# Graph attention on a sparse adjacency matrix: 384 rows ranked early, their q made in part one

## The chip, the cores and the metric

The kernel runs on one core of one Trainium2 chip. The metric is the device time of one execution in microseconds (us). The engines are TensorE (PE, with PEld for its weight loads), VectorE (DVE), ScalarE (ACT), GpSimd (POOL) and SyncE (SP), which here only issues DMAs. Each engine works through a queue of its own in order.

## The reference

`x` is 3327 x 1024 and fp32, `adj` a symmetric 3327 x 3327 matrix of 0 and 1 with ones on the diagonal, about 0.5% of it ones (17 in a row on average).

```python
h = relu(layernorm(x))
f = h @ Wf + bf;  g = h @ Wg + bg        # 1024 x 1024 weights
e = relu(f @ g.T)
scores = where(adj > 0, e, -9e15)
out = x + softmax(scores, axis=1) @ (h @ W + bW)
```

## The kernel before, in words

Only the scores of neighbours are needed. With A = Wf·Wg^T a score is q·h, where q = h_i·A belongs to the row and h to the neighbour. And softmax times (hW + bW) is (softmax times h)·W + bW. So each row needs its list of neighbours, its q (three thirds of 342 columns, the last holding a bias), one dot per neighbour, a softmax, the weighted sum of the same neighbour rows, and one product with W.

**Part one** (to about 240 us) goes over 26 tiles of 128 rows (the last has 127). For each tile the adjacency is loaded; ACT counts its ones (the degrees), POOL multiplies a mask with column numbers (`r<-r,iotaj`, L704), DVE takes the eight largest of each of 16 segments (`MAX8`, L767, function `segments`) and packs them into a list of up to 24 neighbours (`listed`, stored to `pd` through `pay`); what is left over for rows of higher degree goes to `cd` (`cand`, function `store_left`, L747). Besides, each tile of x is normalised (`measured`, `rooted`, `inverted`, `scaled`, `store_h`: the steps of a layer norm on ACT and DVE, then a store by SP to `hd`), and PE multiplies the weights to A (L837), one step of a list per tile. `emptied1` holds the copies that ACT has to make of finished banks, and `empty()` makes them.

At the end of part one the rows are sorted by degree: PE counts with one-hot matrices how many rows of a degree stand before each row (`before`, `after` into `pre`), DVE makes ranks from it, and 26 more matmuls turn ranks into `perm`, the row number at each rank. SP stores the last lists and the last leftover lists after that.

**Part two** goes over 26 tiles of sorted rows, in the order of `ORDER`. `CAPS` holds how many neighbours a tile has at most. The steps of a tile `t` are: `L` fetches its lists, `H` its own rows (both indirect gathers on POOL, made by `gather`, L639); PE turns the rows (`hT`, L1239) and multiplies them by A (`q`, L1246), ACT copies the bias ahead (`fq`) and the thirds behind (`qc`); `G` gathers one neighbour row for each of the 128 rows into one of `ROWS` row buffers; `d` is a dot on DVE (L1259); `S`, `A`, `E`, `Y`, `T` are the softmax. The weighted sum is made in two ways: `s` on DVE (L1312), or `w` on ACT (L1295, scales the row) and `p` on PE (L1299, adds it transposed). `SHARE` says how many of a tile's rows go the second way. Then PE multiplies with W (`W`, L1327), `X` adds x to the result by a gather, `O` scatters the tile to the output. `C` and `F` fetch the leftover lists (`cts`) and find the neighbours in them for the two tiles with more than 24; `x` fetches the x rows of the last tile into a row buffer. `fl` is a flag that all rows fitted their lists (L1361).

The order in each engine's queue is written by a planner when the program is built. `steps_of` lists each step with its engine, its cost, the steps that it waits for and, for some, a time before which it is not to start. `forward` plays them through: an engine that is free takes, of the steps that can run, the one with the lowest rank; `FREE_AT` says when each engine is done with part one. `backward` re-ranks, 30 passes are made, and the best plan sets the queues and the row buffer of each gather. Between engines only semaphores order the work on the chip; a step whose time the planner misjudged holds what stands behind it in its queue.

```python
FREE_AT = {"POOL": 247.6, "PE": 268.5, "ACT": 268.4, "DVE": 246.0, "DMA": 247.0}
...
        add("POOL", 1.31, 1.31, ("L", t), ("M", t - 3), *(("G", t - 3, k) for k in range(CAPS[ORDER[t - 3]] if t > 2 else 0)))
```

## Time and profile before

| what | before |
|---|---|
| three runs | 1223.2, 1229.3, 1235.4 us (median 1229.3) |
| the profiled execution | 1226.98 us, of which the span is 1225.2 |
| mean granted clock of TensorE | 0.966 |
| DVE busy | 1116.6 us, 91% |
| PE busy | 1098.0 us, 90% |
| POOL busy | 942.2 us, 77% |
| ACT busy | 602.7 us, 49% |

The span runs from the first to the last instruction of the profiled execution. An engine counts as busy while an instruction of its own runs; a wait on a semaphore isn't busy. A matmul's end is modelled. In the views, `G<-hd,ps` is an indirect DMA that gathers rows of `hd` by the list `ps` into row buffers, L639 is the line of the helper that makes it, and "<-ACT q L1128" behind a wait names what ended it. The same steps have other lines in the changed kernel: `gather` L656, dots L1400, thirds of q L944 in part one and L1387 in part two.

### The profile page before, as it was taken

The numbers are of one execution on the slowest core, as the hardware profiler recorded it, in microseconds if no ns is written. First come the engines' busy times: TensorE is split into PE (matmuls) and PEld (weight loads), VectorE is DVE, ScalarE is ACT, GpSimd is POOL, SyncE is SP. The second block draws the span as 40 slices with busy tenths as digits, with TensorE's granted clock in tenths as the row PEclk, the third lists the DMA queues.
The fourth block names the chain that finished last, engine by engine and source line by source line (L and its number), as shares of the span: only waits on it lengthen the run. The fifth ranks groups of instructions, "written<-read, shape, count | busy, mean of one in ns | idle before, by whom it ended". The sixth has DMA issues, their size and how long they took to land. (4 is left out here: it accounts for less than half of the span.)

```text
span 1225.2 us, 14006 instructions
## 1 busy us (share of the span) xinstructions
PE 1098.0 (90%) x4508; PEld 697.0 (57%) x4508; DVE 1116.6 (91%) x2191; ACT 602.7 (49%) x924; POOL 942.2 (77%) x677
## 2 busy tenths in 40 slices
PE   2799990799939899899999999999899999999997
PEld 2566660466628466556665666655465656555553
DVE  5999998659898999999999999898999999999983
ACT  6899887325617355436543365443332434333351
POOL 8999997277677787878888878777787888877841
PEclk9899995799979999999999999999899999999999
DMA  9999999689888999989999998888988989998962
GB/s 369 420 398 396 397 356 338 199 318 339 280 259 278 333 308 316 347 273 326 305 331 316 321 310 299 289 285 296 314 285 284 312 275 320 295 315 258 326 183 54
DMA packets 101913, 374.43 MB, mean 306 GB/s; under 512 B 14859, under 2 KB 18602, under 8 KB 98631
## 3 DMA queue, kind: packets, MB, share of 16 engines
q0 software_dynamic: 79584, 286.77, 69.9%
q1 hardware_dynamic: 22246, 86.68, 18.7%
q8 instruction: 37, 0.61, 0.2%
q14 instruction: 46, 0.38, 0.1%
HBM read 344.11 MB, written 29.30 MB: 305 GB/s over the span
## 5 line engine op out<-in xcount | busy, mean ns | idle before, releaser
L639 POOL DMA_INDIRECT G<-hd,ps x454 | 569.2, 1254 | 152.6 <-issue 96.9
L1259 DVE CUSTOM_DVE_ANT_0 junk<-G,q 128x1024 bf16<-128x1024 f32 x468 | 564.2, 1225 | 35.5 <-DMA G<-hd,ps 21.1
L1327 PE MATMUL p_o<-W_sb,yT 128*128 128x512 f32 x832 | 365.7, 593 | 3.7 <-ACT yT L1323 3.7
L1312 DVE SCALAR_TENSOR_TENSOR G<-G,sc 128x1024 f32<-128x1024 f32 (+1 forms) x281 | 354.8, 1263 | 6.1 <-ACT G L1284 5.4
L1246 PE MATMUL p_q<-A_sb,hT 128*128 128x342 f32 x1152 | 350.3, 455 | 8.7 <-ACT p_q L1255 7.3
L1246 PEld LDWEIGHTS p_q<-A_sb,hT 128*128 128x128 f32 x1152 | 214.4, 191 | 117.0 <-issue 10.0
L1327 PEld LDWEIGHTS p_o<-W_sb,yT 128*128 128x128 f32 x832 | 155.1, 189 | 187.9 <-issue 177.1
L1299 PE MATMUL p_y<-ident,G 128*128 128x128 f32 x1552 | 189.3, 276 | 15.1 <-DVE G L1312 8.3
L1299 PEld LDWEIGHTS p_y<-ident,G 128*128 128x128 f32 x1552 | 174.9, 142 | 43.1 <-ACT G L1295 13.5
L704 POOL TENSOR_TENSOR r<-r,iotaj 128x1664 f32<-128x1664 f32 (+3 forms) x50 | 184.0, 3750 | 3.4 <-ACT r L697 3.4
L1295 ACT ACTIVATE G<-G,sc 128x1024 f32<-128x1024 f32 x168 | 179.1, 1137 | 0.1
L837 PE MATMUL ps_A<-WgT,WfT 128*128 128x342 f32 x432 | 129.7, 458 | 2.4 <-ACT WfT L832 2.4
L767 DVE MAX8 cand<-r 128x8 f32<-128x208 f32 (+2 forms) x416 | 118.9, 360 | 4.2 <-POOL r L704 3.6
L1338 ACT ACTIVATE xp<-p_o,rs 128x512 f32<-128x512 f32 x50 | 34.2, 686 | 174.3 <-PE p_o L1327 131.2
L837 PEld LDWEIGHTS ps_A<-WgT,WfT 128*128 128x128 f32 x432 | 81.3, 192 | 42.3 <-ACT WfT L832 2.5
L697 ACT ACTIVATE r<-r 128x3327 f32<-128x3327 int32 (+3 forms) x27 | 77.3, 2864 | 12.1 <-DMA r<-in_adj_dram 12.1
L1252 ACT COPY q<-p_q 128x342 f32<-128x342 f32 x72 | 31.5, 441 | 103.7 <-PE p_q L1246 74.3
L639 POOL DMA_INDIRECT xp<-in_x_dram,perm x25 | 49.4, 1974 | 19.9 <-ACT xp L1338 13.2
L1280 ACT ACTIVATE sc<-sc,nm 128x10 f32<-128x10 f32 (+10 forms) x36 | 10.9, 303 | 106.2 <-DVE nm L1270 86.6
L1242 ACT COPY hT<-p_t 128x512 f32<-128x512 f32 x48 | 27.3, 585 | 72.3 <-PE p_t L1239 42.9
L1323 ACT COPY yT<-p_y 128x512 f32<-128x512 f32 x52 | 30.0, 586 | 59.9 <-PE p_y L1299 59.9
L1345 POOL DMA_INDIRECT out_dram<-xp,perm x25 | 31.3, 1252 | 35.8 <-DMA xp<-in_x_dram,perm 30.9
(147 smaller groups left out, 724.6 us busy)
## 6 DMA issues: line engine op xcount, KB each, us to landing
r<-in_adj_dram SPq DMA_DIRECT2D x24, 1663.5 KB, 13.1
xt<-in_x_dram SPq DMA_DIRECT2D x22, 512.0 KB, 13.6
hd<-xt SPq DMA_DIRECT2D x22, 512.0 KB, 10.5
G<-hd,ps POOLq DMA_INDIRECT x454, 6.1
A_sb<-in_L_gnn_Wg_dram SPq DMA_DIRECT2D x8, 512.0 KB, 17.1
A_sb<-in_L_gnn_Wf_dram SPq DMA_DIRECT2D x8, 512.0 KB, 12.0
W_sb<-in_L_gnn_W_dram SPq DMA_DIRECT2D x8, 512.0 KB, 6.4
cd<-cand SPq DMA_DIRECT2D x25, 64.0 KB, 12.6
```

The source lines that it names most:

```text
L639: return nc.gpsimd.indirect_dma_start(out=to, out_offset=None, in_=table, in_offset=bass.IndirectOffsetOnAxis(ap=idx, axis=0), **kw,)
L697: nc.scalar.activation(r[:n, b:e], a[:n, b:e], AF.Sign, accum_out=to)
L704: eng.tensor_mul(r[:n, b:e], r[:n, b:e], iotaj[:n, b:e])
L767: nc.vector.max(cands[t][:n, s * 8 : s * 8 + 8], r[:n, s * SW : min(N, (s + 1) * SW)])
L837: nc.tensor.matmul(ps[:, :QB], WfTs[c][:, k, :], WgT[:, k, o : o + QB], start=(k == 0), stop=(k == KD - 1))
L1246: nc.tensor.matmul(ps_q[(3 * t + i) % 2][:, :QB], hT[:, k, :], A_sb[:, k, i * QB : (i + 1) * QB], start=False, stop=(k == KD - 1), skip_gr ...
L1259: nc.vector.tensor_tensor_reduce(junks[k % 2], row(t, k), q[:, :D], 1.0, 0.0, op0=ALU.mult, op1=ALU.add, accum_out=scs[t % 3][:, k : k + 1],)
L1295: nc.scalar.activation(g, g, AF.Copy, scale=scs[t % 3][:, k : k + 1])
L1299: nc.tensor.matmul(ps_y[g][:, c, :], of[:, (4 * g + c) * P : (4 * g + c + 1) * P], ident, is_transpose=True, start=((t, g) not in begun an ...
L1312: nc.vector.scalar_tensor_tensor(y, row_k, scs[t % 3][:, k : k + 1], y, op0=ALU.mult, op1=ALU.add)
L1327: nc.tensor.matmul(ps_o[o], yT[:, k, :], W_sb[:, k, o * CB : (o + 1) * CB], start=False, stop=(k == KD - 1), skip_group_check=True,)
L1338: nc.scalar.activation(to, ps_o[o], AF.Copy, scale=rss[t % 3])
```

## The change

Of the first eight tiles (`GROUP`) of part one, the 384 rows with ranks 384 to 767 by degree among themselves are chosen while part one is running (`greater`, `early_ranks`, `early_rows`, at its steps 10 to 12). They are tiles 25, 24 and 23 of the sorted order, and these are the first three of `ORDER`; all other rows are ranked as before, without them. Their lists are fetched by POOL in the middle of part one, their own rows at step 22, and their q is made by PE in the tail of part one: `turns` is a list of turns and thirds, and each `go()` makes the next one and fills banks ahead for two thirds. `QN` is 3, so q is kept for three tiles; `ROWS` is 25, the index buffers `pis` are fixed, and `iotaq` lies in the buffer of W, whose last five parts are loaded later. The 26 rank matmuls of the end stay; in front of them, counting of the last four tiles is made at once (`several`). `measured(22)` is made by DVE instead of ACT, and half of the segments of tile 23 are scanned later. The planner gets new constants and new times, and the tiles have new caps (471 rows in sum instead of 468) and shares (176 instead of 168).

```diff
-CAPS = [37, 25, 23, 22, 21, 21, 20, 20, 19, 19, 18, 18, 17, 17, 17, 16, 16, 15, 15, 15, 14, 14, 13, 13, 12, 11]
-ORDER = [24, 15, *range(15), *range(16, 24), 25]
-SHARE = [9, 11, 18, 12, 10, 9, 10, 8, 7, 7, 8, 8, 5, 8, 4, 4, 4, 4, 3, 3, 3, 2, 3, 0, 5, 3]
+CAPS = [38, 25, 23, 22, 21, 21, 20, 20, 19, 19, 18, 18, 17, 16, 16, 15, 15, 14, 14, 13, 13, 12, 11, 18, 17, 16]
+GROUP = 8
+FROM = 384
+EARLY = 3
+ORDER = [25, 24, 23, *range(15), 16, 17, 18, 15, 19, 20, 21, 22]
+SHARE = [14, 14, 10, 17, 15, 13, 10, 10, 7, 5, 10, 5, 9, 4, 7, 7, 0, 2, 0, 3, 5, 2, 2, 4, 1, 0]
...
+QN = 3
+STORED = 233.0
+Q_AT = [214.0, 229.0, 244.0]
...
-ROWS = 26
+FREED = [16, 17, 1, 2, 3, 4, 5, 21, 22, 0, 23, 24, 6, 7, 20, 8, 9, 10, 11, 15, 18, 19, 12, 13, 14]
+ROWS = 25
...
+PINS = {("H", EARLY): 0.0, ("H", EARLY + 1): 1.0}
+FREE_AT = {"POOL": 207.0, "PE": 241.0, "ACT": 237.0, "DVE": 243.0, "DMA": 207.0}
-FREE_AT = {"POOL": 247.6, "PE": 268.5, "ACT": 268.4, "DVE": 246.0, "DMA": 247.0}
...
-        if t > 1:
-            add("POOL", 1.31, 1.31, ("H", t), row=True)
+        if t >= EARLY:
+            add("POOL", 1.31, 1.31, ("H", t), row=True, at=STORED)
...
-                    *(("d", t - 2, k) for k in range(CAPS[ORDER[t - 2]])), *(("S", t - 2, c) for c in range(2) if i == 2),
+                    *(("d", t - QN, k) for k in range(CAPS[ORDER[t - QN]])),
+                    *(("S", t - QN, c) for c in range(2) if i == 2),
...
-                late = [("F", t)] if k >= KL else [("hc", 2, 1) if k < 6 else ("qc", 2, 1)] if t == 1 else []
-                add("POOL", 1.31, 1.31, ("G", t, k), ("Ld", t), *late, row=True)
+                late = [("F", t)] if k >= KL else []
+                add("POOL", 1.31, 1.31, ("G", t, k), ("Ld", t), *late, row=True, at=STORED)
                 add("DMA", 1.33, 3.2, ("Gd", t, k), ("G", t, k))
                 add(
-                    "DVE", 1.148, 1.32, ("d", t, k), ("Gd", t, k), *(("qc", t, i) for i in range(3)),
-                    ("M", t), at=(256.0, 266.0)[t] if t < 2 else 0.0,
+                    "DVE", 1.148, 1.32, ("d", t, k), ("Gd", t, k), *hs, ("M", t), at=Q_AT[t] if t < EARLY else 0.0,
...
+        def greater():
+            nc.vector.tensor_tensor(
+                more_than,
+                iotad[:, None, :].to_broadcast([P, GROUP, NBIN]),
+                deg[:, :GROUP, None].to_broadcast([P, GROUP, NBIN]),
+                op=ALU.is_lt,
+            )
+            tab = p_mm.tile([P, CB], FP, name="ps_A")[:, : GROUP * NBIN].rearrange("p (t d) -> p t d", d=NBIN)
+            several(tab, range(GROUP))
+            for t in range(GROUP):
+                count(tab, every, more_than[:, t, None, :].to_broadcast([P, GROUP, NBIN]))
+            return tab
...
+            nc.vector.tensor_reduce(col, beyond[:, :, 1:EARLY], AX.X, ALU.add)
+            nc.vector.scalar_tensor_tensor(slot, col, float(-P), apart[:, :, 0], op0=ALU.mult, op1=ALU.add)
...
+        hTs, banks, qs = {}, {}, {}
+
+        def early(j):
+            s = ORDER[j] - NT + EARLY
+            return first[:, s : s + 1]
+
+        def turn(j):
+            hTs[j] = wT.tile([P, KD, P], FP, name="WfT")
+            transposed(hTs[j], W_sb[:, KD - 1 - j, :D])
+
+        def fill(j, i):
+            banks[j, i] = p_mm.tile([P, CB], FP, name="ps_A")
+            nc.scalar.copy(banks[j, i][:, :QB], vb[:, i * QB : (i + 1) * QB])
+
+        def third(j, i):
+            if not i:
+                qs[j] = qpool.tile([P, QW], FP, name="q")
+            for k in range(KD):
+                nc.tensor.matmul(
+                    banks[j, i][:, :QB], hTs[j][:, k, :], A_sb[:, k, i * QB : (i + 1) * QB], start=False, stop=(k == KD - 1),
+                    skip_group_check=True,
+                )
+            emptied1.append(lambda: nc.scalar.copy(qs[j][:, i * QB : (i + 1) * QB], banks[j, i][:, :QB]))
+
+        turns = [(turn, 0)]
+        for j in range(EARLY):
+            turns.append((third, j, 0))
+            if j + 1 < EARLY:
+                turns.append((turn, j + 1))
+            turns += [(third, j, 1), (third, j, 2)]
...
+                if i == NT - 4:
+                    empty()
+                    W_sb = wgpool.tile([P, KD, QW], FP, tag="wg", name="W_sb")
+                    for j in range(EARLY):
+                        gather(W_sb[:, KD - 1 - j, :D], hd[: GROUP * P, :], early(j))
...
+                if i == GROUP + 2:
+                    tab = greater()
+                if i > GROUP + LAG:
+                    if counted > GROUP:
                         after(counted - 1)
                     before(counted)
+                if i == GROUP + 3:
+                    early_ranks(tab)
+                elif i == GROUP + 4:
+                    early_rows()
...
+            def go():
+                empty()
+                step = rest.pop(0)
+                for at in [nxt[1:] for nxt in rest if nxt[0] is third][:2]:
+                    if at not in banks:
+                        fill(*at)
+                step[0](*step[1:])
+
             load_x(last)
             for k in range(2):
                 load_W(k)
             one_hot(late, last)
             one_hot(last, NT)
+            after(counted - 1)
+            tab4 = p_tr.tile([P, 4, P], FP, name="ps_tr").rearrange("p a b -> p (a b)")
+            tab4 = tab4[:, : 5 * NBIN].rearrange("p (t d) -> p t d", d=NBIN)
+            several(tab4, range(NT - 4, NT))
+            go()
...
-            s = 0
-            after(counted - 1)
-            for t in range(counted, NT):
-                before(t)
-                segments(NT - 3, s, s + 4)
-                s += 4
-                placed(t)
-                after(t)
-                if t == NT - 4:
-                    inverted(19)
-                    measured(21, True)
             scaled(18)
             store_left(NT - 4)
             store_h(18)
+            segments(NT - 3, 0, SEG // 2)
+            inverted(19)
             scaled(19)
             store_h(19)
+            go()
             load_W(2)
+            measured(21, True)
...
+            while rest:
+                go()
...
-            for k in range(6, KD):
+            for k in range(4, KD):
...
+            if t < EARLY:
+                gather(pis[t % 3], pd[: GROUP * P, :], early(t))
+            else:
+                gather(pis[t % 3], pd[:, :], perm[:, ORDER[t] : ORDER[t] + 1])
...
```

The next rows are those of POOL's queue where part two begins. The iota is its last work of part one; `xt<-hd,perm` are a tile's own rows in a buffer of part one, `ps` the lists, `cts<-cd` the leftover lists, `G<-in_x` the last tile's x, `G<-hd,perm` a tile's own rows, `G<-hd,ps` neighbour rows. Before:

```order
L928 IOTA iotaq 128x3328
L639 DMA xt<-hd,perm 128x1024 x2
L639 DMA ps<-pd,perm 128x25 x2
L639 DMA G<-hd,perm 128x1024
L639 DMA G<-hd,ps 128x1024 x11
L639 DMA cts<-cd,perm 128x128
```

And POOL's queue at the same place in the changed kernel:

```order
L1071 IOTA W_sb 128x3328
L656 DMA cts<-cd,perm 128x128
L656 DMA G<-in_x_dram,perm 128x1024
L656 DMA G<-hd,perm 128x1024 x2
L656 DMA G<-hd,ps_84 128x1024 x16
L656 DMA G<-hd,ps_85 128x1024 x17
```

The gathers of own rows for the first two tiles and of their lists are gone from here, and the fetch of `cts` and of x moved from behind neighbour rows to the head.

ACT's queue ahead of one of the last stores of normalised rows (`xt<-xt` is the normalising, `lnj` the statistics of the next tile), before:

```order
L741 ACTIVATE xt<-xt,nmr,rstd 128x1024
L727 ACTIVATE lnj,sums<-xt 128x1024
L728 ACTIVATE nmr<-sums 128x1
L730 ACTIVATE lnj,sums<-xt,nmr 128x1024
L731 ACTIVATE rstd<-sums,eps 128x1
```

And ACT's queue there in the changed kernel (`WfT` takes a turned tile, `ps_A<-vb` puts the bias into a bank):

```order
L758 ACTIVATE xt<-xt,nmr,rstd 128x1024
L905 COPY WfT<-ps_tr 128x512 x2
L938 COPY ps_A<-vb 128x342
L744 ACTIVATE lnj,sums<-xt 128x1024
L745 ACTIVATE nmr<-sums 128x1
L747 ACTIVATE lnj,sums<-xt,nmr 128x1024
L748 ACTIVATE rstd<-sums,eps 128x1
```

The copies of a turned tile and a bank's filling have come between two tiles' normalising.

More of the change, by code (lines that the diff above doesn't have):

```diff
@@ L556, in planned @@
     chance = random.Random(seed)
-    begins = [256.0]
+    begins = [243.0]
     for s in ORDER:
@@ L566, in planned @@
     for _ in range(passes):
+        for k in steps:
+            k.rank = k.rank if k.pin is None else k.pin
         edges = forward(steps, rows)
@@ L631, in edge_path @@
     perm = const.tile([P, NT], I32, name="perm")
+    first = const.tile([P, EARLY], I32, name="first")
+    pis = [const.tile([P, PW], I32, name=f"ps{i}") for i in range(3)]
     final = const.tile([P, 1], I32, name="final")
@@ L1177, in edge_path @@
         res = tiles("xp", 2, [P, O])
-        junks = tiles("junk", 2, [P, D], BF)
-        scs = tiles("sc", 3, [P, KM])
-        masks = tiles("mask", 3, [P, KM])
+        junk = tiles("junk", 1, [P, D], BF)[0]
+        scs = tiles("sc", 3, [P, max(CAPS)])
+        masks = tiles("mask", 3, [P, max(CAPS)])
         nms, ls = tiles("nm", 6, [P, 1]), tiles("l", 6, [P, 1])
@@ L1358, in scatter, with worst_of @@
                 nc.gpsimd.drain()
+        def worst_of(_):
+            for ps in ps_o:
+                fresh(ps)
+            nc.tensor.matmul(ps_y[1][0:1, 0, 0:1], worst, onesf, start=True, stop=True)
         def told(_):
```

238 lines of the change are left out of this document (147 added, 91 removed).

## The prediction

> **What bounds the kernel now.** I read the busy shares first, then the span cut into stages, then who waits in part two, then the chain that ended last, and last the turn from part one to part two instruction by instruction.
>
> ```profile
> PE 1098.0 (90%) x4508; PEld 697.0 (57%) x4508; DVE 1116.6 (91%) x2191; ACT 602.7 (49%) x924; POOL 942.2 (77%) x677
> ```
>
> ```profile
> 252.50:284.00 31.50, 31.22 (x119) 20.02 (x118) 24.35 (x48) 14.19 (x23) 25.41 (x21) 1.00 0.90 331
> 284.00:345.00 61.00, 61.00 (x288) 40.16 (x287) 53.89 (x88) 27.92 (x41) 43.23 (x34) 1.00 0.84 284
> 345.00:1203.00 858.00, 806.70 (x3339) 507.03 (x3338) 827.68 (x1242) 366.59 (x573) 658.01 (x507) 0.98 0.89 297
> ```
>
> The first row is the page's busy shares over the whole span, the others are stages of part two: the columns are the stretch, its length, then PE, PEld, DVE, ACT and POOL busy, clock, DMA share, GB/s. From 345 to 1203 DVE is busy 827.7 of 858 us and PE 806.7: both are near their limit, and the DMA engines at 0.89 are not far. DVE's idle time is 7.2 us up to 284, 7.1 to 345 and 30.3 after that. Who it waits for:
>
> ```profile
> DVE junk L1259 <- DMA G<-hd,ps: 21.1, 22, 3.7
> DVE junk L1259 <- ACT q L1128: 9.8, 1, 9.8
> DVE flag L1361 <- PE p_y L1192: 5.3, 1, 5.3
> ```
>
> ```profile
> 1141.60 13.73 PE p_o L1327 x32
> 1155.33 9.20 PE p_q L1246 x32
> ...
> 1186.92 14.00 PE p_o L1327 x32
> 1204.65 14.02 PE p_o L1327 x32
> ```
>
> The first of the two fences gives waits of DVE (us, times, longest), the second the chain that ended last (start, us, what): from 1141 on it is PE's products nearly without a gap. Yet DVE has hardly idle time there either, so an end that comes earlier needs both engines earlier.
>
> The turn between the parts is where the change works:
>
> ```profile
> 220.91 4.51 DVE L767 MAX8 cand<-r 128x8 f32<-128x208 f32 x16
> 227.37 1.11 POOL L639 DMA_INDIRECT xt<-hd,perm  x1 [21.33 <-DVE cand L780]
> 234.47 0.18 DVE L782 TENSOR_SCALAR pay<-held 127x24 int32<-127x24 f32 x1
> 235.74 1.43 SPq L750 DMA_DIRECT2D cd<-cand  x2
> 238.72 0.95 POOL L639 DMA_INDIRECT ps<-pd,perm  x1 [8.97 <-DMA pd<-pay]
> 243.11 0.94 POOL L639 DMA_INDIRECT G<-hd,ps  x1 [0.94 <-DVE mask L1234]
> 244.36 0.94 POOL L639 DMA_INDIRECT G<-hd,ps  x1 [0.30 <-issue]
> 247.48 0.44 ACT L1128 COPY q<-ps_A 128x342 f32<-128x342 f32 x1 [3.14 <-PE ps_A L1108]
> 252.08 0.45 ACT L1128 COPY q<-ps_A 128x342 f32<-128x342 f32 x1 [3.68 <-PE ps_A L1108]
> 252.56 1.23 DVE L1259 CUSTOM_DVE_ANT_0 junk<-G,q 128x1024 bf16<-128x1024 f32 x1 [9.77 <-ACT q L1128]
> 254.90 1.98 POOL L639 DMA_INDIRECT G<-hd,ps  x1 [0.30 <-issue]
> 259.49 2.00 POOL L639 DMA_INDIRECT cts<-cd,perm  x1 [0.30 <-issue]
> 269.43 1.04 PE L1239 MATMUL p_t<-ident,G 128*128 128x128 f32 x8
> ```
>
> The lists of the last rows are done at 234.65, the first neighbour row is asked for at 243.11, and the first dot waits for q until 252.56. A third of a q takes 4.60 us (247.48 to 252.08), a q 13.8.
>
> **The change, part by part.** *Work in part two.* CAPS sums to 471 rows instead of 468, SHARE to 176 instead of 168.
>
> ```profile
> L1259 DVE CUSTOM_DVE_ANT_0 junk<-G,q 128x1024 bf16<-128x1024 f32 x468 | 564.2, 1225 | 35.5 <-DMA G<-hd,ps 21.1 <-ACT q L1128 9.8 <-ACT q L1252 1.8
> L1312 DVE SCALAR_TENSOR_TENSOR G<-G,sc 128x1024 f32<-128x1024 f32 x267 | 344.5, 1290 | 4.7 <-ACT G L1284 4.4
> L1299 PE MATMUL p_y<-ident,G 128*128 128x128 f32 x1552 | 189.3, 276 | 15.1 <-DVE G L1312 8.3 <-ACT G L1295 6.8
> ```
>
> Three more dots cost 3 x 1.205 (564.2 / 468) = 3.6 us, five fewer sums (471 - 26 - 176 = 269 against 274) save 5 x 1.29 = 6.5: DVE has 2.9 us less. PE gets 8 more row sums, 8 x 0.98 (189.3 / 194) = 7.8.
>
> *q in part one (PE).* Before, PE reaches the third tile's transposes at 269.43 with two q done. Afterwards two thirds stand ahead of the 26 rank matmuls, and seven thirds and a turn behind them. If the rank matmuls end near 222 (below), the seven take 222 + 7 x 4.6 + 1 = 255, and four clearing matmuls bring PE to the fourth tile's transposes near 259 with three q done. PE is ahead by 10 + 13.8 - 7.8 = 16 us. Bounds: 5, if rank matmuls and thirds slip together, and 35, if the thirds all fit before 240. The first q is whole near 227, so q stops being what the first dot waits for (9.8 us), and the 5.3 us hole at the flag goes. What is late next is the rows.
>
> *The POOL queue.* Part two now begins on POOL with `cts<-cd`, as the rows of the order in the section on the change show. That fetch moved from behind eleven neighbour rows to the head of the queue. It reads `cd`, whose last store is issued by SP only after the last lists, and everything behind it on POOL, all row gathers, waits with it. The planner lets it go at 207 and thinks of rows from 233 on; the queue doesn't. Before, the last lists were done at 234.65, `pd` landed by 238.72 and `cd`, stored about one us later, by some 240. So: last lists done + 5.5 us, then four issues of 1.25 (243.11 to 244.36), then rows. This eats the time that the early lists save.
>
> *The end of part one.* ACT's rows of the order show a pair of turned copies and a bank's filling between two tiles' normalising that weren't there; the same pair stands once more further up, and on DVE half a segment scan and one statistics pair moved ahead of a reciprocal that ACT waits for.
>
> ```profile
> 193.47 7.38 POOL L704 TENSOR_TENSOR r<-r,iotaj 127x1664 f32<-127x1664 f32 x2
> 200.79 5.25 POOL L928 IOTA iotaq<- 128x3328 bf16 x1
> 208.56 1.04 ACT L727 ACTIVATE lnj<-xt 128x1024 bf16<-128x1024 f32 x1
> 209.96 1.15 ACT L730 ACTIVATE lnj<-xt,nmr 128x1024 bf16<-128x1024 f32 x1
> 212.21 1.28 DVE L713 BATCH_NORM_STATS2 st<-xt 127x6 f32<-127x512 f32 x2
> 217.69 0.44 DVE L735 RECIPROCAL rstd<-rstd 128x1 f32<-128x1 f32 x2 [2.21 <-ACT rstd L731]
> 235.46 0.59 ACT L822 COPY WfT<-ps_tr 128x512 f32<-128x512 f32 x1 [0.27 <-PE ps_tr L821]
> 243.90 0.45 ACT L1103 COPY ps_A<-vb 128x342 f32<-128x342 f32 x1
> ```
>
> ACT gains 4 turned copies of 0.59, 4 fills and a q copy of 0.45 (4.6 us) and loses one statistics pair (1.04 + 1.15 = 2.2); DVE's chain gains half a scan (4.51 / 2 = 2.3) and that statistics pair's 1.28. ACT and DVE wait for each other here (2.21 at the reciprocal), so it adds up: 6.0 us. Bounds: 0, if idle time takes it all, and 10, if each added wait on PE counts too. The new ranking work on DVE (about 20 small steps, 0.2 to 1.3 us each) lies in the middle of part one, minus eight steps it replaces: 0 to 4 us, and I take 0, since DVE's first wait for POOL's keys lies behind it. Six gathers more on POOL in part one (7.5 us) end its keys near 208 instead of 200.85; the scan that reads them starts at 220.91, and the iota behind them ends near 214, just when DVE wants it. If that cover were gone it would cost the same 7.5.
>
> So the last lists are done at 234.65 + 6 = 240.7, `cts` goes at 246.2, rows from 251.2 (before: 243.11). A row takes 6.1 us to land (median of the issues, first row below), so the first dot is at 257, 4.7 us later than before. Rows then come at about 1.5 us:
>
> ```profile
> G<-hd,ps POOLq DMA_INDIRECT x454, 6.1
> ...
> 316.00:334.00 18.00, 14.34 (x13) 1.00 0.91 315
> ```
>
> The second row counts POOL's gathers in a stretch in which DVE had dots alone: 18 / 13 = 1.4 us each, and 2.3 from 254.90 to 259.49 (two gathers). The sixteenth row leaves at 251.2 + 15 x 1.5 = 274, is dotted near 281. By 284 DVE has done 17 dots and a softmax step, 17 x 1.205 + 0.6 = 21 us, where before it had done 24.4 (row 252.5 to 284): 3.4 behind, 0.5 net of the 2.9 us less work.
>
> The Trainium skill, SBUF — State Buffer, section on the two separate sides, says that DVE and GpSimd share a port pair as an exclusive lock, held for a whole instruction, and that a gather's descriptors wait while DVE holds it. By that rule the eleven rows behind the first five would come at 2.3 us, 9 us later than here. The rows agree at 254.90 and not at 316 to 334, where the gathers go on at 1.4; the measured 1.5 stays in the sum.
>
> *Three q buffers, 25 row buffers.* The x row is now held from the start, so 24 buffers turn over instead of 26. What POOL waits for with 26, from 300 to 400:
>
> ```profile
> POOL G L639 <- ACT G L1295: 7.5, 7, 4.9
> POOL G L639 <- DVE G L1312: 7.4, 8, 3.1
> ```
>
> Rows are freed by ACT and PE or by DVE's sums. PE's lead and the larger early shares free them sooner, two buffers fewer later. Bounds for DVE's 37 us of idle time after 284: 12 less (most of the 14.9 goes) or 24 more (below). I take 4 less, nearer to the first, since the only waits on rows that show in DVE's total are 21.1 us.
>
> Sum: +0.5 - 4 = -3.5 us on a profiled execution of 1226.98 (span 1225.2 and 1.8 around it): 1223.5. The median of the runs is 2.3 above that execution; I leave the number at 1224.
>
> **The rivals.** *Faster: the rows aren't late.* Normalised rows had landed when POOL fetched them at 227.37; 6 us later, and with two fetches ahead, rows could start near 236 if `cd` didn't hold them. DVE would go on near 243, 9.5 us before 252.56, without the 5.3 hole and with 2.9 less: -17 on DVE, PE's 16 ahead allows it: 1210. For it: all early lists and q are there. Against: 8.97 us of POOL's wait before was for the list store that SP issues just ahead of `cd`.
>
> *Slower: the row buffers.* With 24 of them POOL waits for a freed row at each place where DVE waits today. If each of the 22 waits lasts one gather longer (about 1.25), DVE loses 24 to 28 us: 1249. It decides when POOL is held by buffers in most tiles; today that is 15 us in the worst 100. For it: early shares of 14, 14, 10, 17, 15, 13 leave DVE with dots alone while rows are scarce, and push sums to the late tiles. Against: PE's lead.
>
> *The port rule* above, for all 51 rows of three tiles: 35 of them at 2.3 instead of 1.5, +28: 1252, or less where DVE starves and lets POOL go.
>
> *The tail of part one slips by 10 or more*: rows from 256, first dot at 262, 5 us more: 1229. For it: each added wait of ACT for PE can hold SP's last stores. Against: PE has little else to do there.
>
> **How the numbers follow.** Forecast 0.42, own range 1214 to 1234; faster 0.29; buffers 0.18; port rule 0.03; tail 0.08. One per cent (12 us) is about what a measurement tells from no change. Faster by more: 0.29 x 0.8 and 0.42 x 0.1, 0.28. Slower by more: 0.18 x 0.75 and 0.03, and the tail's edge, 0.19. Within: 0.53. The range 1205 to 1246 leaves out a fifth of the faster case and half of the buffer case, near 0.17.
>
> **What would show it.** Right: `cts` is POOL's first issue of part two and waits some 15 us for `cd`; first row near 251, first dot near 257 with no wait for q; third q whole near 255; DVE's idle time after 284 at 30 to 37 us. Wrong: a first row before 240; DVE waits on `G<-hd,ps` far from 21 us, above (buffers) or below (PE's lead was worth more than thought); PE idle before 345 small, so that its lead isn't there.

## The result and the profile after

| | before | after |
|---|---|---|
| median of the runs | 1226.5 us | 1276.3 us |
| ratio | | 1.039 (1.032 to 1.046) |
| profiled execution | 1226.98 us | 1279.4 us |

The prediction was 1224, with a range of 1205 to 1246: wrong in its sign and outside its range. In this comparison, and in one later session on chip 12, other engines sometimes went on up to 20 us after the modelled end of the PE work that they waited for. I call these late messages; the last section shows them. Set against each session's own kernel before, they come with some 18 to 24 us more: the loss is 49.7 us here, and 30 to 32 on two chips without them. There the changed kernel takes 1251 to 1254 us (ratios 1.027, 1.024 to 1.030, and 1.023, 1.018 to 1.029, below), and this is the slowdown that the change itself has to explain.

First the page of the changed kernel: busy shares, then the groups of POOL's gathers and DVE's dots (columns: line, engine, operation; busy us, mean ns; idle time before and its main cause).

```profile
PE 1126.1 (88%) x4579; PEld 710.1 (56%) x4579; DVE 1135.1 (89%) x2200; ACT 609.0 (48%) x928; POOL 918.7 (72%) x684
...
L656 POOL DMA_INDIRECT G<-hd,ps x456 | 552.1, 1211 | 223.2 <-issue 96.4
L1400 DVE CUSTOM_DVE_ANT_0 junk<-G,q 128x1024 bf16<-128x1024 f32 x471 | 576.4, 1224 | 42.7 <-DMA G<-hd,ps 34.0
```

DVE is busy 18.5 us longer than before (1116.6), where the prediction had 2.9 us less, and POOL 23.5 us less (942.2) with shorter gathers (1.211 us against 1.254). Next its waits, DVE first, then POOL (us, times, longest):

```profile
DVE junk L1400 <- DMA G<-hd,ps: 34.0, 31, 3.4
DVE flag L1507 <- remote: 23.8, 1, 23.8
...
POOL G L656 <- DVE G L1453: 61.9, 48, 9.2
POOL cts L656 <- issue: 35.5, 2, 35.2
POOL G L656 <- PE p_y L1440: 17.3, 18, 6.2
```

The wait for q is gone, as predicted. In its place stands one of 23.8 us at the flag. POOL's wait for rows that DVE's sums set free has risen from 19.6 to 61.9. The turn between the parts, as a timeline (start us, length, engine, line, operation):

```profile
201.43 11.02 POOL L721 TENSOR_TENSOR r<-r,iotaj 128x1663 f32<-128x1663 f32 x3
207.94 4.63 DVE L1189 TENSOR_TENSOR_SCAN incl<-onesd,short 128x48 f32<-128x48 f32 x1
247.96 0.18 DVE L799 TENSOR_SCALAR pay<-held 127x24 int32<-127x24 f32 x1
250.80 1.80 SPq L1135 DMA_DIRECT2D W_sb<-in_L_gnn_W_dram  x4
252.90 0.99 POOL L656 DMA_INDIRECT cts<-cd,perm  x1 [35.23 <-issue]
257.94 0.94 POOL L656 DMA_INDIRECT G<-hd,ps  x1 [0.30 <-issue]
265.00 0.45 ACT L948 COPY q<-ps_A 128x342 f32<-128x342 f32 x1 [4.16 <-issue]
265.76 0.19 PE L1504 MATMUL p_y<-one 128*1 128x1 f32 x2
275.48 0.15 DVE L1507 CAST flag<-p_y 1x1 int32<-1x1 f32 x1 [23.85 <-remote]
275.70 1.21 DVE L1400 CUSTOM_DVE_ANT_0 junk<-G,q 128x1024 bf16<-128x1024 f32 x1
```

The lists are done at 248.1 instead of the predicted 240.7, `cts` goes at 252.9 instead of 246.2, the first neighbour row at 257.9 instead of 251.2, the ninth third of a q ends near 264.9 instead of 255. The intervals between the first three hold; their start does not. And the first dot, predicted for 257, comes at 275.7, behind the flag's copy. The last three lines also show the late messages: the modelled end of the flag's second matmul is 265.95 and DVE goes on at 275.48.

### The profile page after: what moved, and what is told of

Read it like the earlier page. It is cut to its first block, busy times and chain, and to the rows that moved or that the text cites. A ratio compares the mean times of both kernels' runs of the same rounds, so it can differ in the third digit from the quotient of the medians.

```text
span 1277.7 us, 14426 instructions
## 1 busy us (share of the span) xinstructions
PE 1126.1 (88%) x4579; PEld 710.1 (56%) x4579; DVE 1135.1 (89%) x2200; ACT 609.0 (48%) x928; POOL 918.7 (72%) x684
## 5 line engine op out<-in xcount | busy, mean ns | idle before, releaser
L656 POOL DMA_INDIRECT G<-hd,ps x456 | 552.1, 1211 | 223.2 <-issue 96.4
L1400 DVE CUSTOM_DVE_ANT_0 junk<-G,q 128x1024 bf16<-128x1024 f32 x471 | 576.4, 1224 | 42.7 <-DMA G<-hd,ps 34.0
L1468 PE MATMUL p_o<-W_sb,yT 128*128 128x512 f32 x832 | 387.3, 621 | 25.0 <-ACT yT L1464 15.0
L1453 DVE SCALAR_TENSOR_TENSOR G<-G,sc 128x1024 f32<-128x1024 f32 (+1 forms) x279 | 348.0, 1249 | 10.7 <-ACT G L1425 9.7
L1387 PE MATMUL p_q<-A_sb,hT 128*128 128x342 f32 x1104 | 336.9, 456 | 6.7 <-issue 3.4
L1468 PEld LDWEIGHTS p_o<-W_sb,yT 128*128 128x128 f32 x832 | 162.2, 199 | 221.5 <-issue 200.8
L1387 PEld LDWEIGHTS p_q<-A_sb,hT 128*128 128x128 f32 x1104 | 206.5, 192 | 111.1 <-issue 14.4
L1440 PE MATMUL p_y<-ident,G 128*128 128x128 f32 x1616 | 200.1, 277 | 22.5 <-DVE G L1453 12.1
L1436 ACT ACTIVATE G<-G,sc 128x1024 f32<-128x1024 f32 x176 | 186.7, 1137 | 0.0
L1380 PE MATMUL p_t<-ident,G 128*128 128x128 f32 x184 | 28.5, 284 | 31.7 <-ACT hT L1383 21.1
## 6 DMA issues: line engine op xcount, KB each, us to landing
cd<-cand SPq DMA_DIRECT2D x25, 64.0 KB, 11.2
```

The costliest lines, as they stand in the source:

```text
L656: return nc.gpsimd.indirect_dma_start(out=to, out_offset=None, in_=table, in_offset=bass.IndirectOffsetOnAxis(ap=idx, axis=0), **kw,)
L1387: nc.tensor.matmul(ps_q[(3 * t + i) % 2][:, :QB], hT[:, k, :], A_sb[:, k, i * QB : (i + 1) * QB], start=False, stop=(k == KD - 1), skip_gr ...
L1400: nc.vector.tensor_tensor_reduce(junk, row(t, k), q[:, :D], 1.0, 0.0, op0=ALU.mult, op1=ALU.add, accum_out=scs[t % 3][:, k : k + 1],)
L1436: nc.scalar.activation(g, g, AF.Copy, scale=scs[t % 3][:, k : k + 1])
L1440: nc.tensor.matmul(ps_y[g][:, c, :], of[:, (4 * g + c) * P : (4 * g + c + 1) * P], ident, is_transpose=True, start=((t, g) not in begun an ...
L1453: nc.vector.scalar_tensor_tensor(y, row_k, scs[t % 3][:, k : k + 1], y, op0=ALU.mult, op1=ALU.add)
```

## The experiments

The first four runs are from one chip, on which the changed kernel itself wasn't run; they are set against the kernel before on that chip, by ratio, and against the 1251 to 1254 us of the changed kernel on two other chips. The theory after this look: the turn is late, by the lists, by the flag that stands at the head of DVE's queue and by `cts` at the head of POOL's. The rival: the loss lies in the middle of part two, in the row buffers or in something that wasn't costed. One such thing is in the diff: the change also takes one of two buffers away into which the dots write their products (`junk`, which nobody reads).

**Two junk buffers again in the changed kernel.**

```diff
-        junk = tiles("junk", 1, [P, D], BF)[0]
+        junks = tiles("junk", 2, [P, D], BF)
...
-                junk, row(t, k), q[:, :D], 1.0, 0.0, op0=ALU.mult, op1=ALU.add,
+                junks[k % 2], row(t, k), q[:, :D], 1.0, 0.0, op0=ALU.mult, op1=ALU.add,
```

> The changed kernel with two buffers for the dots' unused products (junk) instead of one, nothing else. Theory A (one buffer makes each dot wait for the end of the dot before): consecutive dots in the changed kernel start 1.266 us apart (median), in the kernel before 1.151; with two buffers they go back to 1.15, 196 such pairs x 0.115 = 22 us less DVE work, 1276 - 22 = 1254, if DVE is what bounds. Theory B (the loss is the late turn and PE, DVE only waits elsewhere): the pitch goes back but DVE waits that much longer for rows and scaled rows, 1270 or more.

Measured: 1262.0 us, 1.032 (1.025 to 1.040). Dots that follow each other start 1.15 us apart again, as before the change, instead of 1.27. Yet the kernel isn't faster than the 1251 to 1254. The groups and DVE's wait in this run:

```profile
L656 POOL DMA_INDIRECT G<-hd,ps x456 | 587.8, 1289 | 174.3 <-issue 93.8 <-DVE G L1453 31.2 <-PE p_y L1440 16.6
...
DVE junk L1400 <- DMA G<-hd,ps: 53.6, 60, 3.2
```

The gathers take 1.289 us, and DVE waits 53.6 us for rows: what the dots gain, the rows take back.

**The flag behind the first tile's dots.** The plan's step `fl` is moved behind the first 16 dots.

```diff
+        put_off([('fl', 0)], ('S', 0, 0))
```

> The changed kernel with the copy of the flag moved behind the first sixteen dots in DVE's queue. Theory A (DVE's late start is the flag's wait for PE): the first row has landed by about 262, so the first dot starts at 262 instead of 275.7; at most 14 us less, about 1265 if half of it is kept. Theory B (PE itself is held up at the turn, from 265 to 289, and DVE must wait for PE's next q and sums anyway): first dot at 262 but the time stays within 5 us of 1276.

**The first rows ahead of `cts` and of the x row.** The same for POOL's two fetches.

```diff
+        put_off([('C', 3), ('x', 25)], ('G', 1, 0))
```

> The changed kernel with the fetch of the leftover lists (cts) and of the last tile's x moved behind the first tile's sixteen neighbour rows in POOL's queue. Theory A (cts at the head holds all rows): own rows leave POOL about 238 instead of 255.5, neighbour rows from about 240 instead of 257.9, and PE has the fourth tile's own rows when the thirds end. DVE still waits for the flag, which PE can give at 266 if PE is not held up: 10 us less, 1266. Theory B (a burst of row gathers holds up PE's finishing messages): the same burst comes 17 us earlier, beside PE's thirds, which then take longer than 4.6 us each; the time stays at 1270 to 1280.

Flag behind: 1250.2 us, 1.026 (1.021 to 1.031). Rows first: 1252.6 us, 1.025 (1.021 to 1.030). Timelines of the two, in this order:

```profile
257.29 0.93 POOL L656 DMA_INDIRECT G<-hd,ps  x1 [0.30 <-issue]
...
263.92 1.23 DVE L1400 CUSTOM_DVE_ANT_0 junk<-G,q 128x1024 bf16<-128x1024 f32 x1 [12.41 <-DMA G<-hd,ps]
```

```profile
239.37 0.99 POOL L656 DMA_INDIRECT G<-hd,perm  x1 [20.95 <-DMA hd<-xt]
252.36 0.94 POOL L656 DMA_INDIRECT G<-hd,perm  x1 [12.00 <-DVE one L1323]
253.61 0.94 POOL L656 DMA_INDIRECT G<-hd,ps  x1 [0.30 <-issue]
...
265.29 0.15 DVE L1507 CAST flag<-p_y 1x1 int32<-1x1 f32 x1 [12.88 <-PE p_y L1504]
```

With the flag out of its way the first dot waits for rows until 263.9; with rows earlier it waits for the flag until 265.3. Two gates end within 1.4 us of each other, so taking one away gains next to nothing: 1250 and 1253 us, against 1251 to 1254 unaltered. The second fence shows a third: with `cts` out of the way POOL could start at 239, but its second gather waits 12.0 us for DVE's last check of the lists. That row buffer lies over memory of part one which this check still reads.

**All three edits.**

> The three edits together: two junk buffers, the flag's copy behind sixteen dots, cts and x behind the first tile's rows. If the three costs are separate and add up: 22 + 23 us (first dot at 252 instead of 275.7) less, about 1231, and no better than the kernel before (1226). If PE's hold-ups in the middle of part two are a cost of their own, 1240 to 1255. If the turn alone matters and the junk buffer doesn't, about 1253.

1260.3 us, 1.032 (1.027 to 1.037); the first dot at 261.5, DVE's waits for rows 66 us. With the second junk buffer it is 8 to 10 us slower than the two runs above, on the same chip and although its first dot is earlier.

**The changed kernel once more,** beside the next three on their chip.

> The changed kernel itself once more, unaltered. In its first profile PE's finishing messages came up to 12 us late at the turn (the flag at 275.5 instead of 266) and in several places later; in the four kernels made from it none did, and two of these, whose edits move the first dot by 10 to 12 us, were 24 to 26 us faster. Theory A (the lateness belongs to the conditions of that session): 1255 to 1266 now, the flag at about 266 and the first dot at 266. Theory B (it belongs to this kernel: a burst of gathers beside an idle DVE): 1271 to 1280 again, flag at 275.

1254.3 us, 1.023 (1.018 to 1.029), first dot at 266.3, no late messages.

**The kernel before with 24 row buffers.**

```diff
-ROWS = 26
+ROWS = 24
```

> The kernel before with 24 row buffers instead of 26, so that its planner makes a plan for 24; nothing else. Theory A (the two row buffers that the change gives up for q and the early x cost what the changed kernel loses after the turn, some 10 us from its first to its last dot): 10 to 15 us slower than before, POOL's waits for freed rows up from 23 us towards 80. Theory B (rows come late for another reason): within 5 us of before.

1248.9 us, 1.018 (1.012 to 1.024). Groups and waits of this run:

```profile
L639 POOL DMA_INDIRECT G<-hd,ps x454 | 594.3, 1309 | 161.7 <-issue 103.3 <-DVE G L1312 25.0 <-DMA G<-hd,ps 6.7
...
DVE junk L1259 <- DMA G<-hd,ps: 46.5, 50, 6.3
POOL G L639 <- DVE G L1312: 41.6, 35, 5.2
```

That is 24.6 us more than before (1224.2), where the two theories had 10 to 15 and under 5. DVE's waits for rows go from 21.1 us in 22 places (the first profile of before, from another session) to 46.5 in 50. So the price of the row buffer rival, 24 to 28 us, was right for the kernel before. Its mechanism was only half right: it let each of 22 waits last a gather longer, but the waits stay as short (0.96 and 0.93 us) and there are more than twice as many.

**The kernel before with one junk buffer.** The reverse of the first edit.

> The kernel before with one buffer for the dots' unused products instead of two, nothing else. Theory A (the 0.12 us that a dot then waits for the dot before lets POOL write its gathers: one gather took 1.20 us on average with one buffer, 1.28 with two, and the changed kernel with two buffers was about 10 us slower than with one): as fast as before or up to 10 us faster, gathers below 1.264 us. Theory B (the wait is DVE's time, and DVE is busy 89% of the time): 179 pairs x 0.115 = 20 us slower.

1220.3 us beside 1224.2: ratio 0.9965 (0.9942 to 0.9987). The only version here that is faster than both kernels, by a third of a per cent.

```profile
L639 POOL DMA_INDIRECT G<-hd,ps x454 | 540.5, 1191 | 181.7 <-issue 87.4
L1259 DVE CUSTOM_DVE_ANT_0 junk<-G,q 128x1024 bf16<-128x1024 f32 x468 | 573.2, 1225 | 23.8 <-DMA G<-hd,ps 8.4
```

Dots follow each other at 1.27 us instead of 1.15, which looks like some 20 us lost over the 179 such pairs of the expectation; but the gathers fall from 1.254 to 1.191 us and DVE's waits for rows from 21.1 to 8.4. The dots were waiting for rows anyway. (The figures of before are from the first profile, of another session.)

**The planner's times mended.** The changed kernel's plan assumes that PE is free at 241, ACT at 237 and DVE at 243. It is planned anew with what the traces show:

```diff
-STORED = 233.0
-Q_AT = [214.0, 229.0, 244.0]
+STORED = 238.0
+Q_AT = [252.0, 252.0, 266.0]
...
-FREE_AT = {"POOL": 207.0, "PE": 241.0, "ACT": 237.0, "DVE": 243.0, "DMA": 207.0}
+FREE_AT = {"POOL": 207.0, "PE": 265.0, "ACT": 256.0, "DVE": 252.0, "DMA": 207.0}
...
-            add("POOL", 1.31, 1.31, ("C", t), ("F", t - 1))
+            add("POOL", 1.31, 1.31, ("C", t), ("F", t - 1), at=256.0)
```

and likewise `fm` (the flag's matmul) at 265, the x row not before 1000, and the first tile's begin at 252. The x row no longer holds a row buffer from the start, so this edit also lets 25 buffers turn over instead of 24.

> The changed kernel with the planner's times set to what its trace shows: PE free at 265 instead of 241, ACT at 256, DVE at 252 instead of 243, rows from 238, q of the three tiles at 252, 252 and 266, cts not before 256, x not before 1000 (so that 25 row buffers turn over). Theory A (the plan was made for a turn that doesn't happen, and its order and two buffers cost the time): first dot at 252 to 256, POOL's waits for freed rows below 60 us, 1225 to 1238. Theory B (the work and its buffers don't fit better, whatever the plan): first dot at 253 but 1245 to 1255, as with the two edits of the turn alone.

1239.4 us, 1.012 (1.007 to 1.017), against 1254.3 for the changed kernel on this chip: about half of the loss is gone. The first dot comes at 263.1, still behind rows that wait 12 us for the list check.

**The turn mended as well.** Besides, the scan's counts are put into PSUM, the last four parts of W are loaded ahead of the last list stores, and the first five row buffers lie where part one has long finished.

```diff
-            incl, table, short = (c1.tile([P, NBIN], FP, name=name) for name in ("incl", "table", "short"))
+            incl, table = (c1.tile([P, NBIN], FP, name=name) for name in ("incl", "table"))
+            short = bank[:, 256 : 256 + NBIN]
...
-        G = tiles("G", ROWS, [P, D])
-        G = [G[i] for i in FREED]
+        G = tiles("G", 5, [P, D]) + tiles("G", ROWS - 5, [P, D])
```

> The kernel with the mended planner times and three more edits at the turn: the ranks' running sum reads its counts from PSUM instead of SBUF; the last four parts of W are loaded ahead of the last tile's list stores instead of behind them; the first five row buffers lie where the normalised x tiles lay, so that two own rows and three neighbour rows don't wait for DVE's last check of the lists. Theory A (from its first dot to its end the kernel with mended times takes 974 us, the kernel before 973, so all that is left of the loss is the later first dot, 263 against 247 to 253): first dot at 250 to 254, 1225 to 1230. Theory B (more is lost later, by 25 buffers): first dot as early, but 1233 or more. The running sum should take 0.3 us instead of 4.6, and the last lists should be done at 243 to 244 instead of 248.

**The scan's counts in PSUM alone.**

> The changed kernel with one edit: the ranks' running sum reads its counts from PSUM instead of SBUF. In the changed kernel that sum took 4.63 us and ended 0.12 us after a multiplication of POOL's had ended; in the kernel before it took 0.25 us and read PSUM. Theory A (with two operands in SBUF DVE waits for POOL's instruction): 0.3 us, and the last lists 4 us earlier. Theory B (the sum is as long whatever it reads): 4.6 us. The whole time: 4 us less at most, 1250.

These two ran on chip 12, with late messages: 1261.9 us, 1.029 (1.023 to 1.035), and 1275.3 us, 1.039 (1.032 to 1.046). As times they say nothing of the edits, so the first of them was repeated elsewhere. For the scan the timeline of the second decides:

```profile
201.46 11.02 POOL L721 TENSOR_TENSOR r<-r,iotaj 128x1663 f32<-128x1663 f32 x3
205.89 0.25 DVE L1190 TENSOR_TENSOR_SCAN incl<-onesd,pre 128x48 f32<-128x48 f32 x1
206.18 6.37 DVE L1191 SCALAR_TENSOR_TENSOR pre<-upto,incl 128x48 f32<-128x48 f32 x1
```

With one operand in PSUM the scan takes 0.25 us beside POOL's multiplication, as it does in the kernel before with one junk buffer (there it starts at 199.55, and POOL multiplies until 200.99). The next operation, with both operands in SBUF, takes the wait instead, 6.37 us, and ends at 212.55, when POOL's multiplications end (201.46 + 11.02 = 212.48). So the edit moves the wait and gains nothing: the lists are done at 247.9 here, 248.1 in the first profile.

**Changed kernel, times mended, turn mended and the kernel before, on one chip.**

> The changed kernel unaltered, on a further chip. It took 1276 us where its profile shows late finishing messages of PE and 1254 where it shows none. Either 1251 to 1260 with the flag at about 266, or 1268 to 1280 with the flag after 269; a time in between would say that the two readings are not two conditions.

> The kernel with the mended planner times once more, beside the changed kernel on the same chip. Theory A (the mended times are worth some 15 us in either condition): 15 us below the changed kernel beside it. Theory B (the 15 us were a matter of the chip): within 5 us of it.

> The kernel with mended times and mended turn once more, now beside the one with mended times alone. Its first dot came at 251.8 instead of 263.1, on a chip with late messages of PE. Theory A (the later first dot is what is left of the loss): 9 to 12 us below the mended times alone, within 5 us of before where PE's messages are not late. Theory B (the earlier start is given back, since rows and PE can't follow): within 4 us of the mended times alone.

> The kernel before, unaltered, with a profile from the same chip. Theory A (the late messages come with the changed kernels only): 1220 to 1230, each finishing message within 0.1 us, the flag about 266, also if the three others show late ones. Theory B (they belong to the chip): late messages here too where the others have them.

| | us | ratio | first dot |
|---|---|---|---|
| before | 1219.8 | 1.001 (0.999 to 1.002) | 247.7 |
| changed | 1251.3 | 1.027 (1.024 to 1.030) | 265.6 |
| times mended | 1236.4 | 1.013 (1.011 to 1.015) | 263.0 |
| turn mended too | 1231.6 | 1.009 (1.007 to 1.012) | 251.9 |

The timeline of the last one at the turn:

```profile
241.37 0.93 POOL L655 DMA_INDIRECT G<-hd,ps  x1 [0.30 <-issue]
...
250.26 0.94 POOL L655 DMA_INDIRECT G<-hd,ps  x1 [5.46 <-DVE r L1285]
251.87 1.22 DVE L1399 CUSTOM_DVE_ANT_0 junk<-G,q 128x1024 bf16<-128x1024 f32 x1
```

Now rows are there before DVE is ready for them, and DVE goes from its list checks into the dots without a gap. The first dot is 11.1 us earlier than with the times alone, the end only 4.8: more than half of what the turn gains is given back later. With the turn mended the change still costs 0.9%, 4.2 us of it at the first dot (251.9 against 247.7), since the lists themselves (done at 248.3, no earlier than without the edit of the scan), and DVE's checks of them, are late.

The decomposition of the change's own loss, from the two profiles of this chip, the changed kernel first. Its first dots, and the stretch from 345 to 1183 (columns as in the prediction), then the same of before:

```profile
265.10 0.19 PE L1504 MATMUL p_y<-one 128*1 128x1 f32 x2
265.33 0.14 DVE L1507 CAST flag<-p_y 1x1 int32<-1x1 f32 x1 [14.23 <-PE p_y L1504]
265.55 1.21 DVE L1400 CUSTOM_DVE_ANT_0 junk<-G,q 128x1024 bf16<-128x1024 f32 x1
...
1210.47 1.22 DVE L1400 CUSTOM_DVE_ANT_0 junk<-G,q 128x1024 bf16<-128x1024 f32 x1
...
345.00:1183.00 838.00, 787.36 (x3227) 490.54 (x3227) 803.35 (x1196) 353.51 (x551) 619.88 (x500) 0.98 0.89 300
```

```profile
247.68 1.23 DVE L1259 CUSTOM_DVE_ANT_0 junk<-G,q 128x1024 bf16<-128x1024 f32 x1 [7.30 <-ACT q L1128]
...
1182.15 1.22 DVE L1259 CUSTOM_DVE_ANT_0 junk<-G,q 128x1024 bf16<-128x1024 f32 x1
...
345.00:1183.00 838.00, 795.26 (x3287) 501.25 (x3288) 810.24 (x1218) 358.34 (x561) 650.94 (x502) 0.98 0.90 301
```

The spans are 1249.4 and 1218.7 us, 30.7 apart. The first dot is 17.9 us later (265.55 - 247.68); from the first dot to the start of the last it takes 944.9 us instead of 934.5, 10.4 more; behind it 2.4 more. So nearly six tenths of the loss lie in the turn. In the middle DVE does less per us (803.4 of 838 against 810.2), and PE too. Between the starts of its first and last dot DVE is busy 898.2 us instead of 893.2, and idle 46.8 instead of 41.2.

## Why the prediction was wrong, by its own steps

**What held.** What bounds the kernel: DVE and PE, both near their limit. That `cts` gates all rows at the head of POOL's queue, that it goes some 5.5 us after the lists (here 252.90 - 248.14 = 4.8), that rows start 5 us after it: all measured as predicted. (Without `cts` ahead, though, rows start only 4.3 us earlier, at 253.6 in the run with rows first, since they wait for the list check.) q stopped being what the first dot waits for.

**"The last lists are done at 234.65 + 6 = 240.7": the step that failed first.** They are done at 248.1, 13.5 us later than before. Five of these are the predicted chain: from the end of the ranking's prefix scan to the lists it takes 30.6 us before and 35.6 after, against 6.0 forecast. The other 8.5 are the later end of this scan, 212.6 instead of 204.0, which the prediction didn't look at. The next lines are the last `hit` of the counting and the scan before, and then the last `hit` in the changed kernel:

```profile
203.28 0.19 DVE L806 SCALAR_TENSOR_TENSOR hit<-pre,oh 127x48 f32<-127x48 f32 x1
203.77 0.25 DVE L1031 TENSOR_TENSOR_SCAN incl<-onesd,pre 128x48 f32<-128x48 f32 x1 [0.29 <-PE pre L801]
```

```profile
199.89 0.21 DVE L889 SCALAR_TENSOR_TENSOR hit<-pre,oh 128x48 f32<-128x48 f32 x1 [0.33 <-PE pre L815]
```

The scan starts 4.2 us later (207.94) and takes 4.4 us longer. The later start isn't the counting's, which is done earlier than before; two sets of statistics, half a segment scan and waits of 0.56 and 1.14 us for x stand between the two now. Nor does the start decide: in all nine profiles with both operands in SBUF the scan starts anywhere from 205.8 to 207.9 and ends each time 0.1 us after POOL's multiplications, at 212.0 to 213.3. So its end, and with it the lists, goes by POOL's keys. The prediction saw these end later, by 7.5 us (measured 11.6, 212.4 against 200.8), and put that at nothing, because the scan of the segments that reads these keys comes later; it named the price if that cover were gone, the same 7.5, but gave it no place in the sum. The cover holds for the data. But the prefix scan, which never reads the keys, has both operands in SBUF now, and doesn't finish while POOL's multiplications run. The Trainium skill says so in SBUF — State Buffer, section on the two separate sides: a DVE operation with two SBUF inputs and a GpSimd operation that reads SBUF lock each other out of a port pair, for a whole instruction. The rows agree, 0.25 us with an operand in PSUM and 4.63 and 6.37 without. They show more than one instruction's wait: the scan, started at 207.94 in the second of three multiplications of 3.7 us (201.43 to 212.45), also sat through the third. The prediction weighed this same rule against the neighbour rows, where it looked at POOL's side, and didn't apply it to the new DVE operations beside POOL's keys.

**"The 5.3 us hole at the flag goes."** It grew. In the kernel before, the copy of the flag stands behind seven dots in DVE's queue; afterwards it is at the head, ahead of all dots, because the planner believes PE free at 241. PE reaches the flag's matmul behind nine thirds of q at 265.1, and 14.2 us of DVE's time go to it (23.8 in the first profile), though only its last 1.4 us aren't a wait for rows as well, as the run with the flag behind shows. The prediction had the order in hand but followed only POOL's queue through the turn. PE's own term, "222 + 7 x 4.6 + 1 = 255", came out at 264.9: the rank matmuls behind the late scan end at 229.4 (the row below), and the thirds and turns behind them take 35.5 us instead of 33.2. So PE's lead, forecast as 16 us, is near the lower bound of 5: in the two profiles of one chip it reaches the fourth tile's transposes at 265.2, where before it reached the third's at 264.6, and 13.8 - 7.8 - 0.6 is 5.4.

```profile
227.49 1.94 PE L815 MATMUL pre<-r 128*128 128x52 bf16 x26 [8.19 <-DVE r L1242]
```

That the flag and the rows end together is why undoing either alone moved nothing.

**"24 buffers turn over instead of 26"; "I take 4 less".** The sign was wrong. DVE's idle time behind 284, which the prediction had 4 us shorter, is 14 us longer: 46.3 us (927.0 - 880.7) against 32.4 (899.0 - 866.6), inside its upper bound of 24. The changed kernel first, then the one before, on one chip, each to its last dot:

```profile
284.00:1211.00 927.00, 868.71 (x3625) 546.63 (x3626) 880.69 (x1326) 404.48 (x619) 671.16 (x543) 0.98 0.88 296
```

```profile
284.00:1183.00 899.00, 852.87 (x3547) 538.02 (x3546) 866.59 (x1305) 382.39 (x596) 694.68 (x535) 0.98 0.89 300
```

Waits of DVE and POOL in the same two:

```profile
DVE junk L1400 <- DMA G<-hd,ps: 29.6, 35, 3.3
...
POOL G L656 <- DVE G L1453: 63.8, 55, 6.0
```

```profile
DVE junk L1259 <- DMA G<-hd,ps: 19.2, 17, 4.2
...
POOL G L639 <- DVE G L1312: 17.6, 23, 3.3
```

DVE's waits for rows rise from 19.2 to 29.6 us, POOL's waits for DVE's sums from 17.6 to 63.8. The second isn't a loss by itself: it is 40.9 us in the kernel before with one junk buffer, the fastest version here, and 67.9 with the turn mended. The rival had the buffers at 24 to 28 us, and in the kernel before that is what two cost. In the changed kernel, the 10.4 us of new waits for rows are less, and the next step is one reason: with two junk buffers these waits were 53.6.

**The junk buffer: a term that the sum didn't have.** One buffer fewer spaces the dots by 0.12 us, which DVE's total shows: 576.4 us for 471 dots instead of 564.2 for 468, so 8.6 beyond the three more. It also shortens POOL's gathers, and pays for itself in the kernel before (1220.3 against 1224.2). In the changed kernel the runs point the same way (1250 and 1253 with one, 1260 and 1262 with two, on one chip), but they differ in other edits too. Of DVE's 18.5 us of new busy time 12.2 are the dots; the sums give 6.8 back (354.8 to 348.0), and the other 13.1 lie outside both, the scan's 4.4 among them.

**The price of lateness, and the chances.** Slower by more than 1% had 0.19. The tail's slip had 0.08, with a first dot at 262 and 1229: it came, with 265.6, 8.6 us behind the forecast of 257. (Against the kernel before on that chip, whose first dot is at 247.7 and not 252.6, it is 17.9 us late where 4.7 were forecast.) But its price was set at one for one, and in the one pair of runs that shows it, a late start costs less than half of its length: with the turn mended the first dot is 11.1 us earlier for 4.8 us of time. The replanned kernel moves the first dot by 2.6 us only, and saves 14.9. What shrinks in its trace are DVE's waits for rows behind the turn: 12.4 us (23.6 less one of 11.2 at the first dot, in the next line), against 29.6; in the pair on the chip before, 10.3 against 33.7.

```profile
DVE junk L1400 <- DMA G<-hd,ps: 23.6, 19, 11.2
```

I read this as the order: a plan made for earlier times puts things that aren't ready at the head of queues, in more places than the turn. The prediction, which quoted the planner's times for POOL alone, had no term for that. But it isn't shown, because the same edit frees a 25th row buffer. Two buffers cost 24.6 us in the kernel before; if one is worth half of that, 12.3 us, which is an estimate, it would explain most of the 14.9. No run separates the two.

**What stays open.** Why PE's messages come late in two sessions, and there in the changed kernels only. Whether POOL's six early gathers could be moved off the path of its multiplications, so that the lists come at the old time, wasn't tried. The replanned kernel with the x row held from the start, which would tell order from buffer, wasn't run either. And with the turn mended, 0.9% remain, of which about 7.5 us lie behind the first dot. Between its first and last dot DVE is busy 5.3 us longer there than in the kernel before (898.5 against 893.2) and idle 1.4 longer, so most of it is work of DVE; how it divides between caps, shares and the junk buffer wasn't measured.

## What to carry to other kernels

Where a queue's order is planned from times of an earlier profile, compare the planner's times with the trace after each change: here a plan with the trace's times, which also freed a row buffer, won back half of a 2.7% loss. When work moves ahead of a sync point, follow every queue through that point, and look at what stands at the head of each; if two gates end together, undoing one shows nothing. And before calling a delay covered because nobody reads its data yet, look for operations that can't finish beside the one that got later, as the scan here (4.63 us instead of 0.25).

## What the runs showed of the hardware that was not expected

Slower dots made a kernel faster, by 0.35% in the kernel before. With gaps of 0.12 us between DVE's dots POOL's gathers take 1.19 us instead of 1.25 in the kernel before, and about 1.2 (1.19 to 1.21) instead of 1.29 in the changed one. The Trainium skill's page SBUF — State Buffer has a mechanism of this kind, in its section on the two separate sides: descriptors for a gather can't be written while a DVE operation in a two-port mode holds the shared port. The direction agrees. But no run here shows that the dots hold that port, or isolates it.

Late messages. In the profile of the changed kernel PE's transposes end at 266.98, as modelled, and ACT's copy of their result starts at 287.43; a wait further on shows the same:

```profile
265.88 1.10 PE L1380 MATMUL p_t<-ident,G 128*128 128x128 f32 x8
...
287.43 0.59 ACT L1383 COPY hT<-p_t 128x512 f32<-128x512 f32 x1 [17.81 <-remote]
...
643.80 0.59 ACT L1464 COPY yT<-p_y 128x512 f32<-128x512 f32 x1 [8.87 <-remote]
```

"Remote" marks waits whose release the trace doesn't hold. In one of the changed kernel's two profiles without late messages the transposes start at 265.22 and this copy at 265.96. Such waits came in two sessions, in the changed kernel and two made from it, never in part one; the kernel before took its usual 1218 to 1235 us in both. The same changed kernel, and the one with the turn mended, ran without them in other sessions, so the kernel alone doesn't bring them; what does stays open. Whether PE really ends late or its message comes late can't be told either, since the ends are modelled.
